# W_v's blocks by other ways, and late q loads on another queue, in an attention layer over sparse neighbours

## The chip, the cores and the metric

The kernel runs on one core of a Trainium2 chip. A core has TensorE (matrix products, called PE in the profile), VectorE (DVE), ScalarE (ACT), GpSimd (POOL) and SyncE (SP, which here only issues transfers). Each takes its own instructions in order, and they wait for one another through semaphores. Transfers between the chip's large memory and the core's own memory run on 16 transfer engines, whoever issues them; SyncE, ScalarE and GpSimd each have a queue of issues. The metric is device time in microseconds (us) of one execution, and the median of several executions is compared.

## The reference

For x of 2708 rows by 1024, an adjacency matrix of 2708 by 2708 with about 4 ones in a row, and three 1024 by 1024 weights with biases:

```python
h = jnp.maximum(_layernorm(x, axis=-1), 0.0)
q = h @ W_q.T + b_q
k = h @ W_k.T + b_k
v = h @ W_v.T + b_v
z = (q @ k.T) / math.sqrt(1024)
z = z * adj
z = jnp.where(z == 0.0, -10000.0, z)
out = x + jax.nn.relu(jax.nn.softmax(z, axis=1) @ v)
```

Everything is in 32-bit floating point.

## The kernel before

Since each row has few neighbours, no 2708 by 2708 product is formed. The kernel multiplies W_q and W_k into one matrix M beforehand, so that a row's scores are products of q = h M with rows of h; the weighted sum u of rows of h is formed next, and only u is multiplied by W_v. The rows are sorted by their number of neighbours, in 21 full tiles of 128 rows and a rest. The neighbours' rows are gathered from memory by index (`gather`, L607; the instruction's line is L610 or L612), one tile of 128 x 1024 for each neighbour slot.

**Products.** Rows go through TensorE in units of two tiles. Units 0 to 9 are "q" units (q = h M for tiles 0 to 19), units 10 to 19 are "o" units (out = u W_v), and one tile is left over for the end. A unit is a product of 2 x 2 blocks of 512 by 512, by Winograd's form of Strassen's method: seven block products in place of eight. The right-hand operand is in blocks M11, M12, M21, M22 (the tile `M`) and four sums T0 to T3 (the tile `T`, a view of `wlow`): T0 = M12 - M11, T1 = M22 - T0, T2 = M22 - M12, T3 = M21 - T1. The left-hand operands a11, a12, a22 and s1 to s4 are made by VectorE (`blocks`, L711; sums at L722 and L742, transposes at L705 for "faced" tiles). The order of a unit (`multiply`, L1045, and `opened`, L1016, which starts the next unit ahead) is: a11 M11 and s1 T0 (both in `opened`, at the end of the unit before), s2 T1, a12 M21, s4 M22, s3 T2, then the next unit's a11 M11 and s1 T0, then a22 T3. All products have the line L1011. Between them stand the calls `after(0)` to `after(6)`, into which all other work of the unit is written. (n, i) below means `after(i)` of unit n; in the code it is counted from the last q unit, `last_q` = 9, so (-1, 0) is `after(0)` of unit 8 and (1, 0) that of unit 10.

**Results.** ScalarE and VectorE read the products out of the accumulator banks. In a q unit VectorE makes c12 (L1095) and c22 (L1092); L1092 reads a bank into which a22 T3 is afterwards accumulated, so TensorE waits there if VectorE is late. The q rows of tiles from 8 on go to `q_late` in memory (L1085), and come back when their scores are due.

**W_v.** M's blocks are replaced by W_v's blocks B11 to B22 while unit 9 is still running. M12 isn't used by any product once the T's are formed, so B12 goes there, placed at (8, 0); B11 goes to M11 at (9, 0); B22 goes to T1 at (9, 2), B21 to M21 at (9, 3) and B22 again to M22 at (9, 4) (loads at L1266, all issued by SyncE, 1 MB each). VectorE then forms T0 = B12 - B11 at (9, 2), T1 = B22 - T0 in place at (9, 4), T2 = B22 - B12 at (10, 0) and T3 = B21 - T1 at (10, 1) (L1270, 128 x 2048 each). From (10, 1) on, M12 is given to the gathers as two more slots beside eleven others.

**Attention.** A generator written in program order (`attention`, L960) is advanced by some 21 us of VectorE work a unit: for each tile the scores (L863, one for a gathered slot), the exponentials, and the weighted sum (L912, L923). `fetch` (L820) brings a tile's q rows into one of two buffers when the scores of an earlier tile are done: by a gather on GpSimd for tiles below 8 (L612), by a plain load on SyncE for later ones (L833), and by half of each for one mixed tile, called SECOND (L831). `fill` (L839) issues gathers of neighbours' rows into free slots; a slot comes free when VectorE or ScalarE has used it. GpSimd issues these gathers, the additions of x to finished rows (L1110) and the scatters of finished rows (L808). Finished u rows go to `u_dram` and come back for their o unit (`load_rows`, L1197; L700).

**Order.** VectorE's instructions are issued as written (`manual_schedule`). From unit 4 on, the order on the other engines and on SyncE is set by the scheduler of the language at build time: it takes what it reckons ready, earlier in the program first, so that something can be issued long before the place where it is written.

Of the kernel before, what the change touches and what calls it, by code (L numbers as in the profile page):

```python
# [14 lines left out]
AF = mybir.ActivationFunctionType  # L15
ALU = mybir.AluOpType
AX = mybir.AxisListType

P = 128
# [10 lines left out]
EARLY = 8  # L30
# [35 lines left out]
def tile_preln_masked_attention(  # L66
# [12 lines left out]
    nc = tc.nc  # L79
# [3 lines left out]
    scale = 1.0 / math.sqrt(D)  # L83
# [11 lines left out]
    HP = P // 2  # L95
# [16 lines left out]
    q_late = dram.tile([(BARE - EARLY) * P, D], FT, name="q_late")  # L112
# [63 lines left out]
    t = 0  # L176
    while t < NT:
# [4 lines left out]
        t = e  # L182
# [17 lines left out]
    M = core.tile([P, 2, 2, 4, NB], FT, name="M")  # L200
# [10 lines left out]
    def row_tile(name):  # L211
        return work.tile([P, D], FT, tag="row", name=name, bufs=ROWS)
# [220 lines left out]
    T = wlow.rearrange("p (k a) (b w) -> p k (a b) w", a=2, b=2)  # L433
# [12 lines left out]
    with tc.tile_pool(name="w", bufs=1, side="left") as wp:  # L446
# [11 lines left out]
        t1 = [work.tile([P, D], FT, tag="hT", name=f"t1_{k}", bufs=2) for k in range(2)]  # L458
# [61 lines left out]
        if True:  # L520
# [13 lines left out]
            for o in range(DC):  # L534
# [4 lines left out]
                else:  # L539
                    k = o - H  # L540
# [18 lines left out]
        Z = [psum.tile([P, NB], FT, tag="acc", name=f"ps_z{i}") for i in range(H)]  # L559
# [44 lines left out]
    def small(name):  # L604
        return half.tile([P, NB], FT, tag="half", name=name, bufs=14)

    def gather(dst, src, t, w, n, skip=False):  # L607
        off = bass.IndirectOffsetOnAxis(ap=ptab.bitcast(U32)[:n, t, w:w + 1], axis=0)
        if skip:
            return nc.gpsimd.indirect_dma_start(out=dst, out_offset=None, in_=src, in_offset=off,  # L610
                                                bounds_check=N - 1, oob_is_err=False)
        return nc.gpsimd.indirect_dma_start(out=dst, out_offset=None, in_=src, in_offset=off)  # L612
# [176 lines left out]
    slots, free = [], []  # L789
# [13 lines left out]
    wanted, g_of, tq, first_q = [], {}, {}, []  # L803
# [11 lines left out]
    def ask(t):  # L815

        g_of[t] = []
        wanted.extend((t, s) for s in range(K[t]))

    def fetch(t):  # L820

        if t not in g_of:
            ask(t)
        if t == BARE:
            return
        assert formed.issuperset(range(EARLY) if t < EARLY or t == SECOND else (t,)), t
        tq[t] = work.tile([P, D], FT, tag="hT", name=f"pq_{t}", bufs=2)
        if t == SECOND:
            assert EARLY in formed
            gather(tq[t][:HP], q_dram[:, :], t, SLOTS - WIDE, HP)  # L830
            nc.sync.dma_start(tq[t][HP:], q_late[:HP, :])  # L831
        elif t >= EARLY:
            nc.sync.dma_start(tq[t], q_late[(t - EARLY) * P:(t - EARLY + 1) * P, :])  # L833
        else:
            got = gather(tq[t], q_dram[:, :], t, SLOTS, P)
            if t == order[0]:
                first_q.append(got)

    def fill():  # L839
        while wanted and free:  # L840
            t, s = wanted.pop(0)
            g = free.pop(0)
            if s == K[t]:
                half = slice(HOSTS.index(t) * HP, (HOSTS.index(t) + 1) * HP)
                nc.gpsimd.dma_start(g[:HP], v_dram[half, :])
            else:
                with tc.issue_after(first_q[0].ins) if first_q else nullcontext():
                    gathered.append(gather(g, h_dram[:, :], t, s, P, skip=True))
            g_of[t].append(g)

    def chained(step):

        with tc.issue_after(chain[-1].ins):
            chain.append(step())
# [64 lines left out]
    def sums(t):  # L919
        u, coef, m = us.pop(t)  # L920
        for s in range(0 if t in EMPTY else 1, K[t]):
            fill()
            chained(lambda: nc.vector.scalar_tensor_tensor(  # L923
                u, g_of[t][s], coef[:, s:s + 1], u, op0=ALU.mult, op1=ALU.add))
            free.append(g_of[t][s])
            yield 1.3
        fill()
        if t in HOSTS:
            chained(lambda: nc.vector.scalar_tensor_tensor(
                u[:HP], g_of[t][K[t]][:HP], m[:HP, 3:4], u[:HP], op0=ALU.mult, op1=ALU.add))  # L930
            free.append(g_of[t][K[t]])
            yield 1.3
            fill()
        g_of.pop(t)
        if t == SECOND:
            nc.sync.dma_start(v_dram, u)
            whole_second.append(True)
            return
        unit = next((n for n, pair in enumerate(units) if pair[0] == "o" and t in pair[1:]), len(units))
        if now < [unit - 2, 2] and unit <= len(q_pairs) + 4 or unit >= len(units) - 1:  # L940
            faced_tiles.add(t)
        print("done", t, "at", now, "unit", unit, t in faced_tiles)
        if t in faced_tiles:
            v = row_tile(f"v_{t}")
            nc.scalar.copy(v.rearrange("p (a c r) -> p c a r", a=QUADS, r=QP),
                           u.rearrange("p (c a r) -> p c a r", a=QUADS, r=QP))
            nc.scalar.dma_start(u_dram[t * P:(t + 1) * P, :], v)
        elif near(t):
            held[t] = u
        else:  # L950
            nc.sync.dma_start(u_dram[t * P:(t + 1) * P, :], u)
        done.add(t)
# [34 lines left out]
    done, held, ws, us = set(), {}, {}, {}  # L987
    formed = set()
    faced_tiles, whole_second = set(), []
# [4 lines left out]
    spent, now = [0.0], [0, 0]  # L994

    def near(t):

        return t == alone or any(t in unit[1:] for unit in units[:now[0] + 3] if unit[0] == "o")
# [10 lines left out]
    def add_block(bank, a, b, last=True):  # L1009
        for c in range(4):  # L1010
            mm = nc.tensor.matmul(bank, a[:, c, :], b[:, c, :], start=False, stop=(c == 3), skip_group_check=True)  # L1011
        return mm
# [3 lines left out]
    def opened(n):  # L1016

        if n not in banks_of:
            return
        X, Z = banks_of[n]  # L1020
        ops = ops_of[n][0]
        add_block(X, ops["a11"], M[:, 0, 0])
        Y = psum.tile([P, NB], FT, tag="acc", name="psy")
        nc.scalar.copy(Y, X)
        products.append(add_block(Z, ops["s1"], T[:, 0]))
        p5 = small("p5")
        nc.scalar.copy(p5, Z)
        opened_of[n] = Y, p5

    def between(n):  # L1030

        if n == len(units) - 1:
            single["first"] = one_started(single["banks"], single["turned"][:, 0:4, :])
        else:
            opened(n + 1)
# [151 lines left out]
    def of_wv(i, j):  # L1187

        return wv[j][:, i * 4:(i + 1) * 4, :]
# [5 lines left out]
    units = [("q",) + p for p in q_pairs] + [("o",) + p for p in o_pairs]  # L1195
# [19 lines left out]
    products = []  # L1215
    last_q = len(q_pairs) - 1
# [10 lines left out]
    single = {}  # L1227

    opened(0)
    for n, unit in enumerate(units):  # L1230
        kind, ta, tb = unit
# [12 lines left out]
        def after(i):  # L1244
# [13 lines left out]
            if n == FIRST and i in (1, 4, 5):  # L1258
                for g in slots[:4] if i == 1 else slots[4:6] if i == 4 else slots[6:8]:
                    with tc.issue_after(sorted_at[-1].ins):  # L1260
                        nc.vector.memset(g, 0.0)
            b11, b12, b21, b22 = M[:, 0, 0], M[:, 0, 1], M[:, 1, 0], M[:, 1, 1]
            for at, place, src in (((-1, 0), b12, of_wv(0, 1)), ((0, 0), b11, of_wv(0, 0)), ((0, 2), T[:, 1], of_wv(1, 1)),
                                   ((0, 3), b21, of_wv(1, 0)), ((0, 4), b22, of_wv(1, 1))):
                if (n - last_q, i) == at:
                    nc.sync.dma_start(place, src)  # L1266
            for at, place, a, b in (((0, 2), T[:, 0], b12, b11), ((0, 4), T[:, 1], T[:, 1], T[:, 0]),
                                    ((1, 0), T[:, 2], b22, b12), ((1, 1), T[:, 3], b21, T[:, 1])):
                if (n - last_q, i) == at:
                    nc.vector.tensor_sub(place, a, b)  # L1270
            if (n - last_q, i) == (1, 1):
                free.extend(M.rearrange("p i j (a c) w -> p i j a (c w)", a=2)[:, 0, 1, a, :] for a in range(2))
            if (n, i) == (FIRST, 5):
                next(stream)
            if (n, i) == (FIRST, 6):
# [39 lines left out]
            if nxt is None and i == 1:  # L1315
                uT = work.tile([P, D], FT, tag="hT", name="T_alone", bufs=2).rearrange("p (c q) -> p c q", q=P)
# [53 lines left out]
    y = work.tile([P, D], FT, tag="q", name="y_alone", bufs=4)  # L1370
    send(gather(y, x, alone, SLOTS, P))
    uT, (X, Z), p1 = single["turned"], single["banks"], single["first"]
    add_block(Z, uT[:, 0:4, :], T[:, 0])
    add_block(Z, uT[:, 4:8, :], M[:, 1, 1])
    nc.vector.tensor_add(p1, Z, p1)
    nc.vector.scalar_tensor_tensor(y[:, hi], p1, 0.0, y[:, hi], op0=ALU.max, op1=ALU.add)
# [9 lines left out]
    with tc.If(some > 0):  # L1386
# [19 lines left out]
        with tc.tile_pool(name="big", bufs=1, side="right") as big, tc.tile_pool(  # L1406
# [25 lines left out]
            for t, (t0, n) in enumerate(tiles):  # L1432
                ht = gen.tile([P, D], FT, tag="ht", name="g_h")
                nc.sync.dma_start(ht[:n], h_dram[t0:t0 + n, :])
                for s in range(DC // 4):
                    pt = psum.tile([P, 4, P], FT, tag="tp", name="g_pt")
                    for c in range(4):
                        k = s * 4 + c
                        nc.tensor.transpose(pt[:, c, :n], ht[:n, k * P:(k + 1) * P], ident[:n, :n])
                    nc.vector.tensor_copy(hT[:, s * 4:(s + 1) * 4, t0:t0 + n], pt[:, :, :n])  # L1440
            with tc.For_i(0, NT) as i:
# [9 lines left out]
                q = gen.tile([P, D + 1], FT, tag="q", name="g_q")  # L1451
# [25 lines left out]
                for b0 in range(0, N, NB):  # L1477
                    w = min(NB, N - b0)
# [84 lines left out]
```

## Time and profile before

| what | us |
|---|---|
| median of three runs | 637.88 (637.53 to 639.61) |
| profiled execution, its own time | 638.0 |
| its span, first to last instruction | 636.3 |
| TensorE busy | 624.6 |
| VectorE busy | 525.7 |
| GpSimd busy | 361.8 |
| ScalarE busy | 283.5 |

All times of the profile are counted from the first instruction. A row of an order of instructions reads: start, duration, engine, line, operation, tile written <- tiles read, count, and in brackets how long the engine stood idle before it and what ended that. A row of a table of stretches reads: the stretch, its length, busy time and number of instructions of TensorE, its weight loads, VectorE, ScalarE and GpSimd, then the clock granted to TensorE, the busy share of the transfer engines, and GB/s. A row on one line of the code reads: shortest, median and longest duration in ns, first and last start in us. The span divides thus: until 105 M is formed, until about 372 run the q units, and then the o units; the last product ends at 627.3.

### The profile page before, as it was taken

What the parts mean: (1) busy time and instruction counts of PE and PEld (TensorE: products, weight loads), DVE (VectorE), ACT (ScalarE), POOL (GpSimd) and SP (SyncE); (2) the same over time, 40 slices, a digit from 0 to 9 for tenths busy, and PEclk for the clock granted to TensorE, in tenths of its full rate; (3) what the DMA queues carried; (4) which work ended last, traced back from release to release, by engine and by line L of the source; (5) the groups of instructions that cost most, each with busy time, mean ns of one, the idle gap of its engine ahead of it and who ended that gap; (6) DMA issues with size and microseconds to landing.
All of it is one profiled execution on the core that took longest, in us unless ns stands there. A gap on an engine that the chain in (4) does not pass through costs nothing.

```text
span 636.3 us, 6139 instructions
## 1 busy us (share of the span) xinstructions
PE 624.6 (98%) x1627; PEld 315.5 (50%) x1627; DVE 525.7 (83%) x1021; ACT 283.5 (45%) x421; POOL 361.8 (57%) x383
## 2 busy tenths in 40 slices
PE   9999999999999999999999999999999999999994
PEld 5777766444444544444444434444444444444441
DVE  5999889897995755997889999999999989898341
ACT  3539975859667533424341243443343333422300
POOL 2649960975868277563742563576566777632431
PEclk9999999999999999999999999999999999999997
DMA  8998897598696439986699998999999999893761
GB/s 339 407 372 310 334 351 298 199 342 328 246 382 221 170 113 334 326 299 196 194 289 323 297 412 216 311 318 324 351 378 321 334 299 295 242 289 95 210 217 40
DMA packets 62352, 180.11 MB, mean 283 GB/s; under 512 B 10039, under 2 KB 17031, under 8 KB 61672
## 3 DMA queue, kind: packets, MB, share of 16 engines
q0 software_dynamic: 25136, 78.41, 39.4%
q1 hardware_dynamic: 31242, 80.19, 35.8%
q10 hardware_dynamic: 5934, 21.06, 8.5%
q8 instruction: 15, 0.25, 0.2%
q14 instruction: 25, 0.20, 0.1%
HBM read 147.23 MB, written 42.31 MB: 298 GB/s over the span
## 4 chain that ended last, share of the span: by engine, by line
PE 85%; DVE 6%; issue 4%; DMA 3%; SPq 1%; POOL 0%; ACT 0%; POOLq 0%; DVEq 0%; ACTq 0%
PE ps L1011 38%; PE psy L1011 28%; PE ps_y L476 6%; PE ps_x L476 4%; PE ps_z L476 4%; PE pt L415 3%; DVE u L923 2%; DMA g<-h_dram,tab 1%; DMA or<-u_dram 1%; DVE junk L863 1%; DVE s L722 1%; DVE wlow L1270 1%; PE ps_y L511 1%; SPq L700 1%; DVE q L1092 0%
## 5 line engine op out<-in xcount | busy, mean ns | idle before, releaser
L610 POOL DMA_INDIRECT g<-h_dram,tab x94 | 121.4, 1291 | 84.4 <-DVE u L923 31.1
L1011 PE MATMUL ps<-M,a 128*128 128x512 f32 x320 | 144.0, 593 | 0.0
L1011 PE MATMUL psy<-wlow,s 128*128 128x512 f32 x320 | 143.9, 592 | 0.0
L863 DVE SCALAR_TENSOR_TENSOR junk<-g,pq 128x1024 uint8<-128x1024 f32 x93 | 113.7, 1222 | 14.0 <-DMA g<-h_dram,tab 10.9
L1011 PEld LDWEIGHTS ps<-M,a 128*128 128x128 f32 x320 | 59.8, 190 | 70.8 <-issue 70.6
L1011 PEld LDWEIGHTS psy<-wlow,s 128*128 128x128 f32 x320 | 59.7, 190 | 70.2 <-issue 69.4
L923 DVE SCALAR_TENSOR_TENSOR u<-g,coef,u 128x1024 f32<-128x1024 f32 x69 | 88.4, 1281 | 6.9 <-ACT u L912 5.8
L389 DVE FIND_INDEX8 at<-ones,adj 128x8 uint32<-128x685 f32 (+1 forms) x88 | 74.5, 865 | 0.0
L1011 PE MATMUL psy<-wlow,a 128*128 128x512 f32 x160 | 72.0, 593 | 1.4 <-DVE q L1092 1.4
L1011 PE MATMUL ps<-M,s 128*128 128x512 f32 x160 | 72.1, 592 | 0.0
L1011 PE MATMUL ps<-wlow,s 128*128 128x512 f32 x160 | 72.0, 593 | 0.1
L368 ACT ACTIVATE sized<-adj 128x2708 uint8<-128x2708 f32 (+1 forms) x22 | 54.3, 2468 | 7.5 <-DMA adj<-in_adj_dram 6.2
L298 POOL TENSOR_TENSOR hsum<-hsum,x 128x256 f32<-128x256 f32 (+1 forms) x56 | 38.7, 729 | 25.6 <-DVE wlow L444 21.2
L1110 POOL DMA_INDIRECT y<-in_x_dram,tab x19 | 34.8, 1832 | 29.1 <-ACT y L1127 15.9
L1011 PEld LDWEIGHTS psy<-wlow,a 128*128 128x128 f32 x160 | 30.3, 190 | 40.0 <-issue 37.1
L1011 PEld LDWEIGHTS ps<-wlow,s 128*128 128x128 f32 x160 | 30.3, 190 | 38.6 <-issue 37.9
L1011 PEld LDWEIGHTS ps<-M,s 128*128 128x128 f32 x160 | 30.3, 190 | 38.1 <-issue 37.4
L912 ACT ACTIVATE u<-g,coef 128x1024 f32<-128x1024 f32 x18 | 20.7, 1147 | 32.1 <-DVE coef L911 32.1
L808 POOL DMA_INDIRECT out_dram<-y,tab x21 | 25.0, 1188 | 16.4 <-DVE flag L1354 6.1
L626 POOL DMA_INDIRECT tab_dram<-tab,pos_i x22 | 21.9, 995 | 20.7 <-DVE pos_i L689 15.3
L276 ACT ACTIVATE x<-x,r 128x1024 f32<-128x1024 f32 (+1 forms) x22 | 25.9, 1235 | 7.3 <-POOL r L266 7.3
L760 ACT COPY ps<-bp_sb 128x512 f32<-128x512 f32 x42 | 24.5, 595 | 7.2 <-DVE y L1145 6.7
(251 smaller groups left out, 843.5 us busy)
## 6 DMA issues: line engine op xcount, KB each, us to landing
adj<-in_adj_dram SPq DMA_DIRECT2D x21, 1354.0 KB, 11.3
x<-in_x_dram SPq DMA_DIRECT2D x21, 512.0 KB, 3.9
h_dram<-x ACTq DMA_DIRECT2D x21, 512.0 KB, 8.7
u_dram<-v ACTq DMA_DIRECT2D x13, 512.0 KB, 6.4
or<-u_dram SPq DMA_DIRECT2D x52, 128.0 KB, 7.0
q_late<-q SPq DMA_DIRECT2D x12, 512.0 KB, 6.0
pq<-q_late SPq DMA_DIRECT2D x12, 512.0 KB, 8.6
M<-in_wv_dram SPq DMA_DIRECT2D x4, 1024.0 KB
```

Of the source, the lines that this page charges most:

```text
L276: nc.scalar.activation(xs[i][:n], xs[i][:n], AF.Relu, bias=r[:n, 4, i:i + 1], scale=r[:n, 3, i:i + 1])
L298: small.append(nc.gpsimd.tensor_add(hsum[:n, cols], hsum[:n, cols], xt[:n, cols]))
L368: nc.scalar.activation(sized[:n], a[:n, :, :PW], AF.Abs, accum_out=total[:n, t:t + 1])
L389: nc.vector.max_index(at[:n, k - first_k, g, :], ones[:n, 0:8], a[:n, g, :])
L476: mm = nc.tensor.matmul(bank, a_tile(o + H * a[0], a[1], i), b(o), start=first and o == 0, stop=(o == H - 1), skip_group_check=True)
L610: return nc.gpsimd.indirect_dma_start(out=dst, out_offset=None, in_=src, in_offset=off, bounds_check=N - 1, oob_is_err=False)
L760: nc.scalar.copy(return_[h], row[:, h * NB:(h + 1) * NB])
L808: to = nc.gpsimd.indirect_dma_start(out=out, out_offset=bass.IndirectOffsetOnAxis(ap=ptab.bitcast(U32)[:n, t, SLOTS:SLOTS + 1], axis=0), i ...
L863: chained(lambda: nc.vector.scalar_tensor_tensor(junk, g_of[t][s], 1.0, tq[t], op0=ALU.mult, op1=ALU.mult, accum_out=zall[:, t, s:s + 1]))
L923: chained(lambda: nc.vector.scalar_tensor_tensor(u, g_of[t][s], coef[:, s:s + 1], u, op0=ALU.mult, op1=ALU.add))
L1011: mm = nc.tensor.matmul(bank, a[:, c, :], b[:, c, :], start=False, stop=(c == 3), skip_group_check=True)
L1110: return nc.gpsimd.indirect_dma_start(out=y[:n], out_offset=None, in_=x, in_offset=off, compute_op=ALU.add)
```

## The change

- B11 is loaded into M12's place (named t1) at (7, 0). At (7, 6) ScalarE negates it in two halves, and GpSimd issues a transfer of B12 from memory that adds to what lies there. So t1 = B12 - B11, which was T0, without VectorE.
- In the o units, and for the single tile at the end, the product s1 T0 takes t1 in M12's place.
- T0's place is therefore free once unit 9's own s1 T0 is done. B22 is loaded there at (9, 0), in place of T1 at (9, 2).
- VectorE forms T1 = T0's place - t1 at (9, 3), in place of (9, 4); T2 = T1 - B11 at (10, 0); T3 as before. Three differences are left of four.
- From (10, 1) on, T0's place is given to the gathers, where it was M12.
- The plain loads of late q rows in `fetch`, twelve of 512 KB and one of 256 KB, are issued by GpSimd, where it was SyncE.
- A print at build time is dropped.

```diff
         if t == SECOND:
             assert EARLY in formed
             gather(tq[t][:HP], q_dram[:, :], t, SLOTS - WIDE, HP)
-            nc.sync.dma_start(tq[t][HP:], q_late[:HP, :])
+            nc.gpsimd.dma_start(tq[t][HP:], q_late[:HP, :])
         elif t >= EARLY:
-            nc.sync.dma_start(tq[t], q_late[(t - EARLY) * P:(t - EARLY + 1) * P, :])
+            nc.gpsimd.dma_start(tq[t], q_late[(t - EARLY) * P:(t - EARLY + 1) * P, :])
...
-        products.append(add_block(Z, ops["s1"], T[:, 0]))
+        products.append(add_block(Z, ops["s1"], T[:, 0] if units[n][0] == "q" else M[:, 0, 1]))
...
-            b11, b12, b21, b22 = M[:, 0, 0], M[:, 0, 1], M[:, 1, 0], M[:, 1, 1]
-            for at, place, src in (((-1, 0), b12, of_wv(0, 1)), ((0, 0), b11, of_wv(0, 0)), ((0, 2), T[:, 1], of_wv(1, 1)),
+            b11, t1, b21, b22 = M[:, 0, 0], M[:, 0, 1], M[:, 1, 0], M[:, 1, 1]
+            for at, place, src in (((-2, 0), t1, of_wv(0, 0)), ((0, 0), T[:, 0], of_wv(1, 1)), ((0, 0), b11, of_wv(0, 0)),
                                    ((0, 3), b21, of_wv(1, 0)), ((0, 4), b22, of_wv(1, 1))):
                 if (n - last_q, i) == at:
                     nc.sync.dma_start(place, src)
-            for at, place, a, b in (((0, 2), T[:, 0], b12, b11), ((0, 4), T[:, 1], T[:, 1], T[:, 0]),
-                                    ((1, 0), T[:, 2], b22, b12), ((1, 1), T[:, 3], b21, T[:, 1])):
+            if (n - last_q, i) == (-2, 6):
+                for h in range(2):
+                    nc.scalar.activation(t1[:, 2 * h:2 * h + 2], t1[:, 2 * h:2 * h + 2], AF.Copy, scale=-1.0)
+                nc.gpsimd.dma_start(t1, of_wv(0, 1), accum_op=ALU.add)
+            for at, place, a, b in (((0, 3), T[:, 1], T[:, 0], t1), ((1, 0), T[:, 2], T[:, 1], b11),
+                                    ((1, 1), T[:, 3], b21, T[:, 1])):
                 if (n - last_q, i) == at:
                     nc.vector.tensor_sub(place, a, b)
             if (n - last_q, i) == (1, 1):
-                free.extend(M.rearrange("p i j (a c) w -> p i j a (c w)", a=2)[:, 0, 1, a, :] for a in range(2))
+                free.extend(T.rearrange("p k (a c) w -> p k a (c w)", a=2)[:, 0, a, :] for a in range(2))
...
-    add_block(Z, uT[:, 0:4, :], T[:, 0])
+    add_block(Z, uT[:, 0:4, :], M[:, 0, 1])
```

More of the change, by code (lines that the diff above doesn't have):

```diff
@@ L941, in sums @@
             faced_tiles.add(t)
-        print("done", t, "at", now, "unit", unit, t in faced_tiles)
         if t in faced_tiles:
```

## The prediction

> **What bounds the kernel now.** I read the page's first part, then TensorE's waits and its order of instructions, then VectorE's. The profiled execution took 638.0 us, 0.12 above the median of the three runs (637.88); its span is 636.3.
>
> ```profile
> span 636.3 us, 6139 instructions
> PE 624.6 (98%) x1627; PEld 315.5 (50%) x1627; DVE 525.7 (83%) x1021; ACT 283.5 (45%) x421; POOL 361.8 (57%) x383
> ```
> ```profile
> PE psy L1011 <- DVE q L1092: 1.4, 1, 1.4
> PE ps_y L511 <- POOL hsum L121: 1.2, 1, 1.2
> ```
> ```profile
> 339.78 3.60 PE L1011 MATMUL ps<-wlow,s 128*128 128x512 f32 x8
> ...
> 363.81 3.60 PE L1011 MATMUL ps<-wlow,s 128*128 128x512 f32 x8
> 368.81 3.70 PE L1011 MATMUL psy<-wlow,a 128*128 128x512 f32 x8 [1.41 <-DVE q L1092]
> ...
> 389.74 3.67 PE L1011 MATMUL ps<-wlow,s 128*128 128x512 f32 x8
> ...
> 609.69 3.60 PE L1011 MATMUL ps<-M,T_alone 128*128 128x512 f32 x8
> ```
> ```profile
> 627.28 0.70 DVE y_alone L1379
> ```
>
> TensorE is idle for 636.3 - 624.6 = 11.7 us. Of these 9.0 lie behind its last product (627.28 to 636.3) and 1.2 ahead of its first; the change touches neither. That leaves 1.5, nearly all in one wait of 1.41 us: at 367.4 the last product of unit 9 must not overwrite a bank until VectorE's addition of L1092 has read it. So no shift of work between queues can win more than about 1.5 us, 0.24%, since the products stay as they are. 0.3% (1.9 us) is about what a measurement of this kernel can tell from no change.
>
> Why VectorE is late there:
>
> ```profile
> 293.68 1.23 DVE L863 SCALAR_TENSOR_TENSOR junk<-g,pq 128x1024 uint8<-128x1024 f32 x1 [3.10 <-DMA g<-h_dram,tab]
> ...
> 352.79 2.28 DVE L1270 TENSOR_TENSOR wlow<-M 128x2048 f32<-128x2048 f32 x1
> ...
> 360.25 2.60 DVE L923 SCALAR_TENSOR_TENSOR u<-g,coef,u 128x1024 f32<-128x1024 f32 x2
> 362.76 0.68 DVE L1095 TENSOR_TENSOR q<-ps,u 128x512 f32<-128x512 f32 x1
> 363.37 2.28 DVE L1270 TENSOR_TENSOR wlow<-wlow 128x2048 f32<-128x2048 f32 x1
> 365.56 2.60 DVE L923 SCALAR_TENSOR_TENSOR u<-g,coef,u 128x1024 f32<-128x1024 f32 x2
> 368.08 0.68 DVE L1092 TENSOR_TENSOR q<-psy,p 128x512 f32<-128x512 f32 x1
> ...
> 388.90 0.69 DVE L722 TENSOR_TENSOR s<-a,s 128x512 f32<-128x512 f32 x1
> ```
>
> Its order is fixed. At 293.68 it waits 3.10 us for a gathered row tile, falls behind TensorE, and from there works almost without a gap to 390. Two differences of W_v (L1270) stand ahead of L1092. The next close place is 388.90: the operand ends at 389.59, and its product starts at 389.74.
>
> **The change part by part.**
>
> *The differences.* Four become three, and ahead of L1092 two become one: the one of 352.79 is gone, the one of 363.37 moves ahead of L1095. Alone, this brings L1092 forward by 2.28 us, to an end of 368.76 - 2.28 = 366.48, before TensorE asks for it at 367.41 (363.81 + 3.60).
>
> *The SECOND tile's half of late q rows, now issued by GpSimd.* It stands between these two gathers:
>
> ```profile
> 282.08 1.72 POOL L612 DMA_INDIRECT pq<-q_dram,tab  x1 [0.67 <-DVE junk L863]
> 284.10 1.91 POOL L610 DMA_INDIRECT g<-h_dram,tab  x1 [0.30 <-DVE q L1092]
> ```
> ```profile
> L845 POOL DMA_DIRECT2D g<-v_dram x2: 573/592/612, 344.2 to 558.7; - x2
> L610 POOL DMA_INDIRECT g<-h_dram,tab x94: 987/1021/3000, 234.7 to 557.1; - x94
> ```
>
> The gather of 284.10 is the one that VectorE awaits until 293.68, so what is put ahead of it counts in full. The nearest row is L845, a plain load of the same 64 rows: 0.59, and 0.30 between two issues, 0.89. Ends: 0, if the tile lands late for the load on the transfer engines (0.84 busy below) whatever the issue; 3.30, by the longest gather. The lead at L1092 is then 2.28 - 0.89 = 1.39; it ends at 367.37, in time, and the wait of 1.41 goes. At the next close place TensorE could start at 389.74 - 1.41 = 388.33; VectorE is ready at 389.59 - 1.39 = 388.20. Gain 1.41. With a load of 3.30 the lead is -1.02, and the step loses 1.02; with 0 the gain is still 1.41.
>
> *B22's first load, earlier.* SyncE's queue now:
>
> ```profile
> 219.26 0.33 SPq L1266 DMA_DIRECT2D M<-in_wv_dram  x1
> ...
> 281.88 0.49 SPq L831 DMA_DIRECT2D pq<-q_late  x1
> ...
> 339.97 0.33 SPq L1266 DMA_DIRECT2D M<-in_wv_dram  x1
> 349.27 0.33 SPq L1085 DMA_DIRECT2D q_late<-q  x1
> ...
> 350.27 0.63 SPq L1266 DMA_DIRECT2D wlow<-in_wv_dram  x1
> ```
>
> T0's place is free when the product of 339.78 ends, at 343.4, and SyncE is free then, so I put the issue there. No row shows a landing; the load of 350.27 was read at 363.37 without a wait, so it takes at most 13.1 us, which gives 356.5 at the latest. The difference moved ahead would start near 360.25 - 2.28 = 357.97. Cost 0; if the issue comes only behind the store of 349.27, up to 349.6 + 13.1 - 357.97 = 4.7 us.
>
> *B11, its negation, and the adding transfer of B12.* The row of 219.26 is a load placed in unit 9's neighbourhood and issued four units earlier, as soon as its place was free. I expect B11 there, the negation behind it, and the adding transfer from about 231 on.
>
> ```profile
> L375 ACT ACTIVATE junk_m<-M x8: 1057/1064/1082, 205.8 to 224.2; 128x1024 uint8<-128x1024 f32 x8
> ```
> ```profile
> 247.40 1.28 DVE L722 TENSOR_TENSOR s<-a,pt 128x512 f32<-128x512 f32 x2 [3.23 <-ACT a L718]
> ```
> ```profile
> 229.00:232.00 3.00, 3.00 (x9) 1.33 (x8) 1.82 (x2) 0.31 (x1) 3.00 (x13) 1.00 0.23 23
> 255.00:283.00 28.00, 28.00 (x78) 13.24 (x77) 25.94 (x46) 11.76 (x19) 15.07 (x13) 1.00 0.89 308
> 283.00:298.00 15.00, 15.00 (x45) 7.19 (x44) 10.54 (x19) 4.71 (x7) 5.71 (x5) 1.00 0.84 265
> 369.00:390.00 21.00, 20.94 (x49) 9.14 (x49) 19.37 (x39) 8.40 (x15) 9.26 (x7) 1.00 0.87 337
> 484.00:521.00 37.00, 37.00 (x104) 17.48 (x103) 35.09 (x57) 12.83 (x23) 27.08 (x22) 1.00 0.97 312
> ```
>
> Negating two halves is 2 x 1.06 us of ScalarE, which is busy 0.31 of the 3 us from 229 to 232: cost 0, at most those 2.1 if a copy for TensorE stands behind. The transfer adds 1.05 MB that the kernel did not move before; at 308 GB/s (row 255 to 283) that is 3.4 us of the transfer engines, and if adding needs two passes, 6.8. From 231 on it meets engines 0.23 busy, and at 247.40 VectorE still waits 3.23 us for an operand that TensorE paces, which swallows that much delay. I take 0; ends 0 and 6.8, the upper if it runs right ahead of 284 to 296. The transfer's own issue on GpSimd is one more instruction of 0.6 to 3.0.
>
> *The other twelve late q loads.*
>
> ```profile
> L833 SPq DMA_DIRECT2D pq<-q_late x12: 319/320/433, 373.8 to 525.0; - x12
> ```
> ```profile
> 500.99 1.23 DVE L863 SCALAR_TENSOR_TENSOR junk<-g,pq 128x1024 uint8<-128x1024 f32 x1 [0.96 <-DMA g<-h_dram,tab]
> ...
> 551.48 2.61 DVE L923 SCALAR_TENSOR_TENSOR u<-g,coef,u 128x1024 f32<-128x1024 f32 x2 [1.62 <-ACT u L912]
> 564.34 0.69 DVE L1122 TENSOR_TENSOR p<-taken,p 128x512 f32<-128x512 f32 x1 [0.95 <-ACT taken L1076]
> 576.93 3.92 DVE L923 SCALAR_TENSOR_TENSOR u<-g,coef,u 128x1024 f32<-128x1024 f32 x3 [1.22 <-ACT u L912]
> 605.03 1.25 DVE L705 STREAM_TRANSPOSE T_alone<-or 128x1024 f32<-128x1024 f32 x1 [11.56 <-DMA or<-u_dram]
> ```
>
> Each waits on GpSimd until VectorE has left the buffer, with the next tile's gathers, additions of x and scatters queued behind. Each costs GpSimd 0.89 (L845) to 3.30. From 369 to 390 GpSimd is busy 9.26 of 21 us, so the first ones find room. In 484 to 521 it is busy 27.08 of 37 us plus 22 spaces of 0.30, so 3.3 us are left, and VectorE already waits for a gather (500.99). Some four loads fall near there: 3.6 to 13.2 us, of which I take 3.6 as VectorE's delay. Behind it VectorE has 1.62 + 0.95 + 1.22 = 3.79 us of waits to give back, and the last operand (605.03 + 1.25 = 606.28) stands 3.41 ahead of its product at 609.69: 7.2 us of cover. Cost 0; at the upper end 13.2 - 7.2 = 6.0. SyncE gets the time free, and nobody on the path waits for it: gain 0.
>
> As to a rule: the Trainium skill, page "DMA: Bandwidth & Descriptors", section "SWDGE vs HWDGE vs iDMA", would leave plain loads on SyncE or ScalarE, since GpSimd writes its descriptors in software, and VectorE's two-port operations lock it out of the memory they lie in. The spread of L610 from 987 to 3000 ns agrees that such issues are sometimes held up, though no run here shows by what. By that rule the sum would go with the longest gather, 639.0.
>
> *The freed places* (T0's for M's second block) come in the same number and step: 0.
>
> Sum: 638.0 - 1.41 + 0 = **636.6 us**; its own range is 636.2 to 637.3.
>
> **The rivals.**
>
> *Gain eaten:* GpSimd's issue ahead of 284.10 costs about 2.3, the lead is gone, the 1.41 stays: 638.0. For it: POOL rows of 1.72 and 1.91 at that very place. Against: L845.
>
> *Slower, the adding transfer late:* GpSimd issues it not at 231 but between 255 and 287, when the transfer engines are 0.89 busy. The gather of 284.10 lands 3.4 to 6.8 later; with 0.89 for the q load and 2.28 back, TensorE loses 2.0 to 5.4 more: 640.0 to 643.4, 640.5 taken. It decides from a delay of 2.28 + 1.9 = 4.2 us at 293.68. For it: the program writes it in unit 7, far later; against: the load of 219.26.
>
> *Slower, GpSimd full near 500:* a delay over 7.2 us makes the last product wait: up to 636.6 + 6.0 = 642.6; 640 taken.
>
> *B22 not sooner:* the issue stays behind 349.27, VectorE waits up to 4.7, of which the lead pays 1.39: 638.0 + 4.7 - 1.39 = 641.3 at the worst, 639.5 taken.
>
> **How the numbers follow.** Forecast 0.52, gain eaten 0.12, adding transfer late 0.19, GpSimd full 0.11, B22 not sooner 0.06. Faster by over 0.3% (below 636.0) needs the whole forecast and a run's spread on top: 0.11, all from the forecast. Same: 0.41 of the forecast, the eaten gain's 0.12 and 0.02 of B22's: 0.55. Slower (above 639.8): 0.34. The range 635.8 to 640.6 leaves out about half of the slower cases.
>
> **What would show it.** Right: no wait at L1092 near 367 and three L1270, the second ahead of L1095; a plain load behind 282.08 with the next gather 0.9 later; the adding transfer before 255. Wrong: a wait of VectorE for gathers over 4 us near 293; GpSimd without a pause from 464 and a product at 610 that waits; VectorE waiting for wlow near 358.

## The result, and the profile after

| | before | changed |
|---|---|---|
| median, us (22 runs each, side by side) | 638.27 (637.31 to 640.12) | 637.2 (636.81 to 638.39) |
| profiled execution, its own time | 638.0 | 636.92 |
| its span | 636.3 | 635.2 |
| TensorE's last product read by VectorE at | 627.28 | 625.45 |

The ratio is 0.9987, with a 95% interval of 0.9981 to 0.9993: a gain of 1.07 us, within the 0.3% that the prediction called no change. The profiled execution of the changed kernel fell by 1.08 us. In it TensorE finished 1.83 us sooner, and 0.75 us of that were given back behind its last product.

Line numbers of the changed kernel: products L1010 (L1011 before), c22 L1091 (L1092), c12 L1094 (L1095), W_v's loads L1265, negation L1268, adding transfer L1269, differences L1273 (L1270 before).

The page of the changed kernel, first the span and the busy times, then the only wait of TensorE that the table of waits lists:

```profile
span 635.2 us, 6138 instructions
PE 624.2 (98%) x1627; PEld 316.4 (50%) x1627; DVE 523.9 (82%) x1020; ACT 285.9 (45%) x423; POOL 367.3 (58%) x397
```
```profile
PE ps_y L511 <- POOL hsum L121: 1.2, 1, 1.2
```

The wait of 1.4 us for L1092 is gone. TensorE's order around that place, and VectorE's order, changed kernel:

```profile
363.95 3.60 PE L1010 MATMUL ps<-M,s 128*128 128x512 f32 x8
367.38 3.60 PE L1010 MATMUL psy<-wlow,a 128*128 128x512 f32 x8
```
```profile
292.04 1.22 DVE L863 SCALAR_TENSOR_TENSOR junk<-g,pq 128x1024 uint8<-128x1024 f32 x1 [1.28 <-DMA g<-h_dram,tab]
...
295.17 1.23 DVE L863 SCALAR_TENSOR_TENSOR junk<-g,pq 128x1024 uint8<-128x1024 f32 x1 [1.89 <-DMA g<-h_dram,tab]
...
357.44 2.28 DVE L1273 TENSOR_TENSOR wlow<-wlow,M 128x2048 f32<-128x2048 f32 x1
...
365.26 0.68 DVE L1091 TENSOR_TENSOR q<-psy,p 128x512 f32<-128x512 f32 x1
...
602.46 1.25 DVE L705 STREAM_TRANSPOSE T_alone<-or 128x1024 f32<-128x1024 f32 x1 [11.97 <-DMA or<-u_dram]
...
625.45 0.69 DVE L1382 SCALAR_TENSOR_TENSOR y_alone<-ps,y_alone 128x512 f32<-128x512 f32 x1 [1.95 <-PE ps L1010]
```

One difference (357.44) stands ahead of L1091 instead of two. L1091 ends at 365.94, and the product that needs its bank follows the one before it at 367.38 without a gap: a lead of 1.44 us where there was a lag of 1.41. VectorE's waits for gathered rows between 284 and 297 are 1.28 + 1.89 = 3.17 us, against 3.10 + 0.94 = 4.04 before; the second of these before was:

```profile
295.85 1.23 DVE L863 SCALAR_TENSOR_TENSOR junk<-g,pq 128x1024 uint8<-128x1024 f32 x1 [0.94 <-DMA g<-h_dram,tab]
```

Of the 2.82 us by which L1091 ends sooner (365.94 for 368.76), 0.68 were there ahead of any difference of W_v: the weighted sum at 350.98 before starts at 350.30.

GpSimd's order around the issues that are new to it, SyncE's issue of B22, and the group of the twelve late loads (shortest, median and longest ns, first and last start in us):

```profile
283.00 0.91 POOL L612 DMA_INDIRECT pq<-q_dram,tab  x1 [0.30 <-issue]
284.22 1.94 POOL L610 DMA_INDIRECT g<-h_dram,tab  x1 [0.30 <-DVE q L1091]
286.16 0.60 POOL L831 DMA_DIRECT2D pq<-q_late  x1
287.06 1.59 POOL L610 DMA_INDIRECT g<-h_dram,tab  x1 [0.30 <-issue]
```
```profile
343.54 0.33 SPq L1265 DMA_DIRECT2D wlow<-in_wv_dram  x1
348.59 0.33 SPq L1084 DMA_DIRECT2D q_late<-q  x1
```
```profile
L833 POOL DMA_DIRECT2D pq<-q_late x12: 572/588/605, 354.7 to 532.4; - x12
```
```profile
L1269 POOL DMA_DIRECT2D M<-in_wv_dram x1: 1035/1035/1035, 251.7 to 251.7; - x1
...
DMA to landing us min/median/max: 13.2/13.2/13.2
```

Where the 0.75 us went is seen in the group of the program's last line, whose rows are the closing of each engine's queue. First the kernel before, then the changed one; of three DRAINs of GpSimd's sequencer the longest is the one that counts:

```profile
L1559 POOLq DRAIN  x3: 46/109/6362, 628.8 to 635.7; - x3
```
```profile
L1562 POOLq DRAIN  x3: 46/109/7122, 627.2 to 634.9; - x3
```

A DRAIN is an instruction of the sequencer, which is not counted as busy time. GpSimd's long one follows its last scatter, and the last closing instructions of the other engines start only when it is done (at 635.2 us before, at 634.3 in the changed kernel). This took 6.36 us before and 7.12 in the changed kernel: 0.76 longer, which is the 0.75 that were given back.

### The profile page after: what moved, and what is told of

Its sections match the earlier page's. It is cut to its first block, busy times and chain, and to the rows that moved or that the text cites. A ratio compares the mean times of both kernels' runs of the same rounds, so it can differ in the third digit from the quotient of the medians.

```text
span 635.2 us, 6138 instructions
## 1 busy us (share of the span) xinstructions
PE 624.2 (98%) x1627; PEld 316.4 (50%) x1627; DVE 523.9 (82%) x1020; ACT 285.9 (45%) x423; POOL 367.3 (58%) x397
## 4 chain that ended last, share of the span: by engine, by line
PE 98%; POOL 0%; DVE 0%; POOLq 0%; issue 0%
PE ps L1010 45%; PE psy L1010 32%; PE ps_y L476 6%; PE ps_z L476 4%; PE ps_x L476 4%; PE pt L415 4%; PE ps_y L511 1%; PE ps_h L1222 0%; PE ps_v L594 0%; DVE y_alone L1382 0%; POOL out_dram L1366 0%; POOLq L1388 0%; POOL hsum L121 0%; PE ps_all L680 0%; PE ps_in L678 0%
## 5 line engine op out<-in xcount | busy, mean ns | idle before, releaser
L610 POOL DMA_INDIRECT g<-h_dram,tab x94 | 119.6, 1272 | 62.1 <-ACT u L912 19.1
L1010 PE MATMUL ps<-M,a 128*128 128x512 f32 x320 | 144.0, 593 | 0.0
L1010 PE MATMUL psy<-wlow,s 128*128 128x512 f32 x320 | 143.9, 593 | 0.0
L1010 PE MATMUL ps<-M,s 128*128 128x512 f32 x240 | 107.9, 593 | 0.0
L1010 PEld LDWEIGHTS ps<-M,a 128*128 128x128 f32 x320 | 59.9, 190 | 70.7 <-issue 70.0
L1010 PEld LDWEIGHTS psy<-wlow,s 128*128 128x128 f32 x320 | 59.8, 190 | 70.0 <-issue 69.1
L1010 PEld LDWEIGHTS ps<-M,s 128*128 128x128 f32 x240 | 45.6, 190 | 57.1 <-issue 55.9
L1010 PE MATMUL psy<-wlow,a 128*128 128x512 f32 x160 | 71.9, 593 | 0.0
L1109 POOL DMA_INDIRECT y<-in_x_dram,tab x19 | 32.7, 1723 | 30.5 <-ACT y L1126 15.7
L1010 PEld LDWEIGHTS psy<-wlow,a 128*128 128x128 f32 x160 | 30.5, 190 | 38.2 <-issue 37.5
L1010 PE MATMUL ps<-wlow,s 128*128 128x512 f32 x80 | 36.0, 592 | 0.0
L944 ACT COPY v<-u 128x1024 f32<-128x1024 f32 x13 | 13.6, 1046 | 32.5 <-DVE u L923 28.2
L476 PE MATMUL ps_y<-wlow 128*128 128x512 f32 x64 | 27.6, 593 | 0.0
```

Of the source, the lines that this page charges most:

```text
L476: mm = nc.tensor.matmul(bank, a_tile(o + H * a[0], a[1], i), b(o), start=first and o == 0, stop=(o == H - 1), skip_group_check=True)
L1109: return nc.gpsimd.indirect_dma_start(out=y[:n], out_offset=None, in_=x, in_offset=off, compute_op=ALU.add)
```

## The experiments

There are two theories of the gain, and one of the loss. *Theory A*: the gain comes from one VectorE difference fewer ahead of c22, and the late q loads on GpSimd give nothing. *Its rival*: the late loads matter, by the gathers or by SyncE's freed time. *Of the loss*: it lies in GpSimd's DRAIN, and the DRAIN depends on what GpSimd issued. The kernels of the experiments were measured on three chips; each is compared with runs of the kernel before on its own chip (medians 637.96, 638.22 and 640.38 us).

### W_v's part alone, and the q loads alone

```diff
 # wv_only: the changed kernel with the loads back on SyncE
-            nc.gpsimd.dma_start(tq[t][HP:], q_late[:HP, :])
+            nc.sync.dma_start(tq[t][HP:], q_late[:HP, :])
...
-            nc.gpsimd.dma_start(tq[t], q_late[(t - EARLY) * P:(t - EARLY + 1) * P, :])
+            nc.sync.dma_start(tq[t], q_late[(t - EARLY) * P:(t - EARLY + 1) * P, :])
 # q_only: the kernel before with just these two lines on GpSimd
```

> The change with the late q loads left on SyncE; W_v's part as changed. Theory A, one difference fewer ahead of L1091 wins the time: TensorE's wait of 1.41 us near 367 is gone, L1091 ends near 366.5, the last product ends 1.5 to 1.8 us earlier than before (627.2), GpSimd's last drain takes some 6.4 us as before, and the time is 1.5 to 1.8 us below before, lower than with the whole change. Rival B, what wins is SyncE's queue being free of the q loads, or the mixed tile's load standing behind its first gather: a wait of 0.7 us or more stays near 367, and the time lies within 0.7 us of before. On the end: if the drain of some 7.1 us seen with the whole change comes from GpSimd's additional transfers, it is back at 6.4 here; if it comes from anything else, it stays at 7.1.

Measured: 636.17 us, ratio 0.9977 (0.9965 to 0.9988).

> The kernel before with only the late q loads moved to GpSimd; four differences as before. Theory A: the wait at L1092 near 367 stays, shortened to about 0.7 us by the 0.7 us that VectorE already gained at 301 in the changed kernel; four L1270. With a drain of 7.1 us at the end the time is equal to before or up to 0.5 us longer. Rival B: no wait near 367, and 1 us less than before.

Measured: 638.42 us, ratio 1.0007 (0.9998 to 1.0016). The closing group in both, wv_only first:

```profile
L1562 POOLq DRAIN  x3: 46/170/6400, 626.9 to 634.3; - x3
```
```profile
L1559 POOLq DRAIN  x3: 46/109/7022, 627.8 to 635.4; - x3
```

The whole gain is W_v's part; the loads on GpSimd gain nothing. The DRAIN goes with the loads: 6.36 and 6.40 without them, 7.12 and 7.02 with them. The intervals of wv_only and of the changed kernel overlap a little, and they were measured on different chips; that the changed kernel is slower than wv_only by some 0.7 us rests on these rows together with the gains in the medians (1.79 and 1.07 us).

One surprise in q_only. In its profiled execution VectorE's wait for a gather (first fence) was 1.72 us and not 3.10, and TensorE (second) did not wait for L1092 although all four differences were there:

```profile
293.81 1.23 DVE L863 SCALAR_TENSOR_TENSOR junk<-g,pq 128x1024 uint8<-128x1024 f32 x1 [1.72 <-DMA g<-h_dram,tab]
```
```profile
364.01 3.60 PE L1011 MATMUL ps<-wlow,s 128*128 128x512 f32 x8
367.53 3.70 PE L1011 MATMUL psy<-wlow,a 128*128 128x512 f32 x8
```

So the stall of 1.41 us belongs to the differences and the gather wait together. In six profiled executions (before 4.04, changed 3.17, wv_only 1.06, q_only 1.72, and below after_again 2.03 and acc_late 2.63) the gather waits between 284 and 298 add up to quite different sums. That q_only's profiled execution had neither the long wait nor the stall is a single observation. It took 637.36 us, 1.1 below the median of that kernel, and the median shows no gain of the loads.

### The differences, dosed

```diff
 # dose1 (range(1)) and dose2 (range(2)): the changed kernel, and at (9, 2)
+            if (n - last_q, i) == (0, 2):
+                for _ in range(2):
+                    nc.vector.tensor_sub(T[:, 1], t1, b11)
```

> The changed kernel with one more difference of 128 x 2048 on VectorE ahead of L1091 (its result is overwritten before any use). Theory A, one for one: L1091 ended at 365.94 and TensorE could ask at 367.55, a margin of 1.61; 2.28 us more give a wait of 0.7 us there, and 0.7 to 1.0 us more in the end: 637.9. Rival B: no wait, 636.9 to 637.2.

Measured: 637.95 us, one execution. TensorE's order:

```profile
368.18 3.70 PE L1010 MATMUL psy<-wlow,a 128*128 128x512 f32 x8 [0.41 <-DVE q L1091]
```

> The same with two more differences (4.56 us). Theory A: a wait of 4.56 - 1.61 = 2.95 us at L1091, and some 3 us more in the end: 640.1. Rival B: below 638.5.

Measured: 640.45 us, one execution. The added differences on VectorE, and TensorE's order:

```profile
352.46 4.61 DVE L1272 TENSOR_TENSOR wlow<-M 128x2048 f32<-128x2048 f32 x2
```
```profile
370.75 3.70 PE L1010 MATMUL psy<-wlow,a 128*128 128x512 f32 x8 [0.47 <-DVE q L1091]
...
391.58 0.70 PE L1010 MATMUL ps<-M,s 128*128 128x512 f32 x1 [1.68 <-DVE s L722]
```

The added differences are overwritten by the real one, and only their time counts. The first 2.28 us of VectorE use up the lead of 1.44 and bring back a stall of 0.41 and a time 1.0 above the profiled 636.92. Of the 2.5 us more that dose2 takes, 0.5 are a wait at 150.7, far ahead of the edit. The 2.0 that remain are what the next 2.3 us of VectorE cost, part at L1091 and part at the operand of the next unit. The wait of 2.95 us at L1091 that the expectation named did not come: in dose2's order four products of the next unit stand ahead of the one that waits. So the times fit theory A, a lead near 1.5 us and behind it nearly one for one, with one execution of each dose.

A stall costs more than the wait in its brackets. Groups of eight products that follow one another without a gap are listed with 3.60 us but start 3.43 apart, so that their listed spans overlap. In dose1 the group ahead of L1091's wait starts at 364.18 and the next at 368.18, 4.00 apart: 0.57 lost, where the row says 0.41. The group that waited is listed with 3.70 us and not 3.60, and the one behind it starts 3.54 later, which loses another 0.11.

### The adding transfer, late

The prediction's dearest rival had the adding transfer run just ahead of the gathers near 284.

```diff
 # acc_late: wv_only, and in fill, ahead of the 20th gather
+                if len(gathered) == 19:
+                    nc.gpsimd.dma_start(M[:, 0, 1], of_wv(0, 1), accum_op=ALU.add)
 # B11 is loaded and negated at (4, 0); acc_284 puts the line under
+                    with tc.issue_after(gathered[18].ins):
```

> The kernel of wv_only (late q loads issued by SyncE, 636.17 us), with the adding transfer of B12 put where the prediction's first rival had it: B11 is loaded into t1 at (8, 0) in place of (7, 0), negated at once, and the adding transfer stands in GpSimd's order directly ahead of the two gathers of rest rows and the gather of q rows that come before the gather of a neighbours' tile at 284. The rival (its 1 MB takes 3.4 to 6.8 us of the transfer engines and 1.0 us of GpSimd just when VectorE waits for gathers): VectorE's waits for gathers between 284 and 297 grow from 1.06 us to between 4.5 and 7.9, L1091 moves from 364.6 to 368.0 to 371.4, TensorE waits there for 1.7 to 5.1 us less what stays of the margin of 1.6, so a time of 638 to 641. The other theory (the transfer runs in time that the queue has to spare): the waits stay under 2.5 us, no wait of TensorE at L1091, and 636.2, give or take 0.6.

Measured: 636.6 us, ratio 0.9974 (0.9965 to 0.9984). It did not test the rival. GpSimd issued the transfer where it had stood all along:

```profile
L848 POOL DMA_DIRECT2D M<-in_wv_dram x1: 1032/1032/1032, 252.4 to 252.4; - x1
```

The scheduler takes what is ready, so writing it later did not move it. What the expectation says of its place is therefore wrong (and B11's load, which it puts at (8, 0), is written at (4, 0) in the code and was issued at 219.9, as good as in the changed kernel, 219.4). The run is a second measurement of wv_only, which it repeats.

> As acc_late was meant: the kernel of wv_only with the adding transfer of B12 tied behind the gather at 280, so that in GpSimd's order it stands directly ahead of the three gathers of neighbours' rows that VectorE waits for between 287 and 297 (the q gather of the SECOND tile then comes behind those three). The rival of the prediction (1.0 us of GpSimd and 3.4 to 6.8 us of transfer engines at that place): VectorE's waits for gathers between 284 and 300 grow from 1.06 us in wv_only to between 4 and 8, L1091 moves from 364.6 to between 367.5 and 371.5, TensorE waits there for 1.3 to 5.3 us, time 637.5 to 641.5 beside 636.2 of wv_only. The other theory (the queue has that much to spare): waits under 2.5 us, no wait of TensorE at L1091, 636.2 give or take 0.5.

Measured: 641.66 us, ratio 1.0013 (0.9994 to 1.0032), on the chip where the kernel before takes 640.38. All four kernels profiled on that chip also wait 1.9 to 2.2 us at L415 (L417 in those with added lines) near 201 for a gather, far ahead of the edit, so rows13 of the next part, which has the same W_v part and was measured beside it, is the kernel to compare with. VectorE's waits for gathers near 300 in acc_284, then in rows13:

```profile
299.54 1.23 DVE L866 SCALAR_TENSOR_TENSOR junk<-g,pq 128x1024 uint8<-128x1024 f32 x1 [5.53 <-DMA g<-h_dram,tab]
...
301.71 1.23 DVE L866 SCALAR_TENSOR_TENSOR junk<-g,pq 128x1024 uint8<-128x1024 f32 x1 [0.94 <-DMA g<-h_dram,tab]
```
```profile
297.02 1.23 DVE L869 SCALAR_TENSOR_TENSOR junk<-g,pq 128x1024 uint8<-128x1024 f32 x1 [2.13 <-DMA g<-h_dram,tab]
...
299.21 1.23 DVE L869 SCALAR_TENSOR_TENSOR junk<-g,pq 128x1024 uint8<-128x1024 f32 x1 [0.96 <-DMA g<-h_dram,tab]
```

GpSimd's and TensorE's order in acc_284:

```profile
286.36 1.03 POOL L849 DMA_DIRECT2D M<-in_wv_dram  x1
287.69 1.78 POOL L610 DMA_INDIRECT g<-h_dram,tab  x1 [0.30 <-DVE q L1094]
```
```profile
372.55 1.98 PE L1013 MATMUL psy<-wlow,a 128*128 128x512 f32 x4 [1.76 <-DVE q L1094]
```

There VectorE waits 6.47 - 3.09 = 3.38 us longer, and TensorE's wait at c22 is back with 1.76 us, beside none in rows13; another of 0.58 stands at 319. These are one execution of each. The waits for gathers range from 1.06 to 4.04 us in the six executions listed above, so that 6.47 is outside what chance showed, but the size of 3.4 is rough. The medians lie only 1.03 us apart (641.66 and 640.63). Two things that are seen in the profiles narrow them: rows13's DRAIN is 0.67 us longer, and in its profiled execution the clock granted to TensorE fell to 0.83 in the stretch from 200 to 210, behind the wait near 201, where acc_284 kept 1.00 (TensorE is busy for 626.0 us in rows13, 624.7 in acc_284). The rival's mechanism is real and its lower price (3.4 us) was about right. It didn't happen in the changed kernel, where the transfer is issued at 251.7.

### What the closing DRAIN depends on

Four kernels add stores to wv_only that nothing reads, so that GpSimd issues more transfers and moves hardly more bytes; the late q loads stay on SyncE.

```diff
 # rows39; rows13 and rows26 have range(1) and range(2); small39 stores one row: zall[:1, ...]
+        asked[t] = len(asked)
+        for i in range(3 if t >= EARLY or t == SECOND else 0):
+            nc.gpsimd.dma_start(idles.pop(), zall[:128, list(asked)[-4], :])
```

> The kernel of wv_only, and at each of its 13 late q loads (which stay on SyncE) GpSimd issues three stores of one row of 64 bytes each to memory that nothing reads: 39 transfers more on GpSimd, with one piece each. Theory 1 (GpSimd's closing DRAIN grows with the number of transfers that it issued, (7.12 - 6.40) / 13 = 0.055 us each): the DRAIN is 6.40 + 2.15 = 8.5 us and the stretch behind TensorE's last product about 11.3. Theory 2 (it grows with the pieces, 128 a load, or with the bytes): 6.4 to 6.5 us and a stretch of 9.2. Theory 3 (6.4 or 7.0 by chance of the execution): either value, and the run of after_again need not show 7.0.

> As small39, but each of the 39 stores has 128 rows of 64 bytes. Theory 1 (number of transfers): again 8.5 us of DRAIN. Theory 2a (pieces): 8.5 us here and 6.4 in small39. Theory 2b (bytes: 39 x 8 KB are less than one late q load): 6.4 in both. Theory 3: 6.4 or 7.0 whatever is issued.

> The changed kernel once more, for a second reading of its closing DRAIN. Theories 1 and 2 (13 late q loads more on GpSimd): 7.0 us, give or take 0.15, and a stretch of 9.7 behind TensorE's last product. Theory 3 (chance of the execution): 6.4 is as likely as 7.1. As to VectorE's wait for gathers between 284 and 297: 3.17 us last time; if it belongs to the order of the issues, it is 3 us again, and if it is chance of the execution, anything from 1 to 4.

Measured: small39 658.89, rows39 633.18, after_again 637.17 us, one execution each. The longest of GpSimd's DRAINs (the third figure, ns), in this order:

```profile
L1568 POOLq DRAIN  x3: 46/109/2549, 653.5 to 656.9; - x3
```
```profile
L1568 POOLq DRAIN  x3: 46/109/3662, 626.9 to 631.1; - x3
```
```profile
L1562 POOLq DRAIN  x3: 46/109/6987, 627.6 to 635.2; - x3
```

None of the theories had this: with 39 transfers more in rows39 the DRAIN is not 8.5 us and not 6.4, but 3.66, and the kernel takes 3.0 us less than wv_only took on another chip, about as much as the DRAIN lost. The changed kernel repeats its 7.0. So the length is no chance of the execution, and it does not simply grow.

> The kernel of wv_only, and at each of its 13 late q loads (which stay on SyncE) GpSimd issues one store of 128 rows of 64 bytes to memory that nothing reads: 13 transfers more on GpSimd, as many as the changed kernel has, with 1.6% of their bytes. If the closing DRAIN depends on the number of GpSimd's transfers (200 gave 6.40, 213 gave 6.90 to 7.12, 239 gave 3.66 and 2.55): 7.0 us, and a time of 636.8. If it depends on their bytes: 6.4 and 636.2. If on what GpSimd does otherwise: neither need come out.

> As rows13, with two stores at each place: 226 transfers of GpSimd. If the DRAIN works off what has gathered since GpSimd last did so, and that is done whenever a fixed number has gathered, it rises by 0.05 us a transfer and falls back at some number between 213 and 239: here either 7.6 us (not yet fallen back, time 637.4) or about 3.0 (fallen back, time 632.6). If it falls steadily with more transfers between 213 and 239: about 5.3.

> The kernel of rows39 once more, with 39 such stores, for an interval: it took 633.18 us in one execution, with a DRAIN of 3.66 us beside 6.40. If the DRAIN belongs to the program, 3.7 us again and 633.2 to 633.6, some 2.8 us less than wv_only; if it was chance, 636 to 637 and 6.4 to 8.5.

Measured, beside 640.38 for the kernel before: rows13 640.63, ratio 0.9998 (0.9980 to 1.0016); rows26 635.11, ratio 0.9916 (0.9890 to 0.9941); rows39_again 635.94, ratio 0.9926 (0.9900 to 0.9953). The DRAIN of rows13 came out as the count of transfers said, its time did not: wv_only's gain less the longer DRAIN would have left it 1.1 us below the kernel before. In its profiled execution the fall of the clock described above accounts for about as much, 1.3 us of busy time; rows39_again has the same fall (626.2 us busy), rows26 has not (624.7). Their closing groups, in this order:

```profile
L1568 POOLq DRAIN  x3: 46/109/7070, 631.2 to 638.8; - x3
```
```profile
L1568 POOLq DRAIN  x3: 46/109/3081, 629.9 to 633.6; - x3
```
```profile
L1568 POOLq DRAIN  x3: 46/109/3660, 631.0 to 635.2; - x3
```

GpSimd's transfers, counted in the trace, beside the DRAIN:

| transfers | kernels | DRAIN, us |
|---|---|---|
| 199, 200 | before; wv_only, acc_late, acc_284 | 6.36; 6.40, 6.41, 6.40 |
| 212, 213 | q_only; changed (twice), dose1, dose2, rows13 | 7.02; 7.12, 6.99, 6.90, 6.96, 7.07 |
| 226 | rows26 | 3.08 |
| 239 | rows39 (twice); small39 | 3.66, 3.66; 2.55 |

From 200 to 213 it rises by 0.5 to 0.7 us, 0.05 a transfer, whether these are loads of 512 KB or stores of 8 KB: bytes don't matter. Nor do packets, the pieces that a transfer is cut into: the queue that GpSimd's transfers use (q0 of the pages) has 25280 of them in wv_only, 1808 more in the changed kernel and only 416 more in rows13, with the same DRAIN (7.12 and 7.07). From 226 to 239 it rises by 0.58 again. Between 213 and 226 it falls by 4.0. A saw tooth of this kind fits a clearing up that is done in between whenever enough has gathered, with the rest left for the end; no run shows that clearing itself, and four counts do not settle the shape. The number is not all of it, since small39 has 239 transfers too, and as many packets as rows39 (26528), and 2.55 us.

small39 was slow for another reason. VectorE's waits for gathered tiles (total, times, longest), small39 and then rows39:

```profile
DVE junk L869 <- DMA g<-h_dram,tab: 26.5, 12, 4.8
```
```profile
DVE junk L869 <- DMA g<-h_dram,tab: 12.5, 6, 5.4
```

With stores of a single row the gathers landed later (9.5 us after their issue in the median, 8.3 in rows39). TensorE then waited, 15.9 us for ScalarE, which itself waited for VectorE's scores, and 2.3 us for VectorE; its granted clock fell to 0.93 in the stretch from 520 to 570, and it was busy for 632.4 us in place of 624.2. Why one row is worse than 128 is open. The pages show one difference. They count 11303 packets under 512 bytes in small39 and 10679 in rows39, 39 x 16 fewer, so that each store goes as 16 packets of data either way (and not as one piece, as the expectation says): of 512 bytes in rows39, of 4 bytes in small39.

rows26 beats both kernels: its ratio is 0.9916 against the changed kernel's 0.9987, with intervals far apart, though the two were measured on different chips. It computes the same, and its 26 stores serve only to shift the number of transfers.

## Why the prediction was right

The forecast of 636.6 stands beside 636.92 in the profiled execution and 637.2 in the median, and a change of less than 0.3% was given the best chance. The mechanism, one difference fewer ahead of c22, was right. That the number came so close is in part luck: two errors of opposite sign hide in the difference of 0.3, since TensorE gained 1.83 and not 1.41, and the tail took back 0.75.

- *The differences.* Right. Predicted end of c22 366.48 without the q load and 367.37 with it, measured 365.94. The wait is gone, three differences are left, wv_only has the gain alone, and the doses show the lead. Of the lead, the 0.68 us that stood ahead of the differences was not forecast; the gather waits of this execution were 0.87 us shorter, so that it is luck as far as the runs show. The gain was under-sized. Up to the stall the changed kernel's products run 0.14 us later (363.95 for 363.81), so from there to the end it gains 1.83 + 0.14 = 1.97 and not 1.41. The prediction read the stall from the brackets; the starts show all of it. Before, the products of 363.81 and 368.81 start 5.00 apart in place of 3.43, which is 1.57; the next start is 0.11 late, the one of 389.74 0.23 (the close place, where no wait was listed), and the one behind it 0.08.
- *The SECOND tile's load on GpSimd.* The place was wrong: the scheduler put it behind the gather of 284.22 and not ahead of it. Its size (0.60 for 0.59) was right, and it cost TensorE nothing there. Whether VectorE's second wait, 1.89 us beside 0.94 before, is its doing is not shown.
- *B22's first load.* Right: issued at 343.54, where 343.4 was forecast, ahead of the store of 348.59, and read at 357.44 without a wait.
- *B11, negation, adding transfer.* Cost 0 was right. The negation ran at 227.4, as early as expected, but in GpSimd's order the transfer stood behind the first gathers, so that its issue came at 251.7 and not from 231 on, only three microseconds inside the 255 named as the bound. acc_284 shows that the rival was a matter of place: some 35 us later VectorE waits 3.38 us longer and TensorE waits 1.76. The rival's condition named the stretch from 255 to 287 as one; only its end was tried.
- *The twelve late q loads.* Cost 0 up to the last product was right, but not by the working: each issue took 0.57 to 0.61, VectorE's last operand came sooner (602.46 for 605.03), and nothing of the 3.6 us of delay showed. q_only shows no gain, as said of SyncE's freed time.
- *The tail.* This is the step that failed: "the change touches neither" of the 9.0 us behind the last product and the 1.2 ahead of the first. Thirteen transfers more on GpSimd (and one for the adding transfer) made the closing DRAIN 0.76 us longer, and rows13 shows as much with idle stores in their place. That is two fifths of what TensorE gained. With it fails the limit of 1.5 us that the prediction set to any shift of work between queues. The stall alone was worth 1.97, and rows26, whose DRAIN is 3.3 us shorter than wv_only's, gained 5.27 us in the median.
- *The rule.* The Trainium skill, page "DMA: Bandwidth & Descriptors", section "SWDGE vs HWDGE vs iDMA", would have left the plain loads on SyncE. wv_only agrees in the sign (636.17 beside 637.2, ratios 0.9977 and 0.9987). The cause was not the held-up issue that the prediction priced at 639.0: the issues took 572 to 605 ns, and the price fell due in the DRAIN.

## What to carry to other kernels

A stretch behind the last product is not fixed because no instruction of the change lies in it: look at what the engines' queues do there, and count GpSimd's transfers, since here 13 more than wv_only's 200 made the DRAIN 0.5 to 0.7 us longer and 26 more made it 3.3 shorter. Price a stall by the starts of the products and not by the idle time beside the row: here the two were 1.57 and 1.41. Work that is off the path until it falls into one narrow place (the adding transfer at 252 or at 286) should be priced by place, and the place read from the order that the scheduler makes, not from where the line is written. A stall that a queue of gathers helps to make varies from one execution to the next, so take its lead from doses rather than from one profile.

## What the runs showed of the hardware that was not expected

- GpSimd's closing DRAIN took 2.5 to 7.1 us and changed with the number of its transfers as a saw tooth would: 6.40 at 200, 7.07 at 213, 3.08 at 226, 3.66 at 239, the same to 0.01 us in two executions of rows39. Stores of one row gave 2.55 at 239.
- A transfer of 1 MB that adds to what lies in the core's memory took GpSimd 1.03 us to issue and landed after 13.2 us; put ahead of awaited gathers it made VectorE wait 3.4 us longer for them in one execution.
- After a wait of TensorE the next group of eight products took 3.70 us in place of 3.60 (at 368.81 before, at 368.18 in dose1), and the loss by the starts was larger than the listed wait.
- Behind a wait of 2.1 us near 201 the granted clock was 0.83 from 200 to 210 in rows13; behind one of 2.2 us at the same place it stayed 1.00 in acc_284.
- With 39 stores of one row of 64 bytes each the kernel was 26 us slower than with 39 stores of 128 such rows (658.89 and 633.18, one execution each).
